# Column halves for the full-width products of layer-1 cross-attention, one more addition on GpSimd ahead of its sums, and four column groups for the layer-3 keys

## The chip, the cores and the metric

The kernel runs on one core of a Trainium2 chip. The metric is the time of one execution on the device, in microseconds (us), from the first to the last instruction and what lies around them; lower is better. The core has five engines with queues of their own: TensorE (PE in the profile; its weight loads are listed apart as PEld), VectorE (DVE), ScalarE (ACT), GpSimd (POOL) and SyncE (SP, which issues transfers).

## The reference, cut to what matters

The reference is a Perceiver-like stack of four layers, each with a cross-attention to a long context, a self-attention and a feed-forward part, on x of 2 x 256 x 256 and a context of 2 x 4096 x 256. The change touches two of its twelve parts, the cross-attentions of layers 1 and 3:

```python
def _L1_xattn_ref(input_query, input_key, input_value, Wq, bq, Wk, bk, Wv, bv, Wo, bo):
    q = jnp.einsum('bsd,hdk->bhsk', input_query, Wq) + bq[None, :, None, :]   # 16 heads of 64
    k = jnp.einsum('bsd,hdk->bhsk', input_key, Wk) + bk[None, :, None, :]
    v = jnp.einsum('bsd,hdv->bhsv', input_value, Wv) + bv[None, :, None, :]
    score = jax.nn.softmax(jnp.einsum('bhqk,bhsk->bhqs', q, k), axis=-1)
    z = jnp.einsum('bhqs,bhsv->bhqv', score, v)
    z = jnp.transpose(z, (0, 2, 1, 3)).reshape(z.shape[0], z.shape[2], -1)
    return z @ Wo + bo

x = x + _L1_xattn_ref(_layernorm(x), ctx, ctx, ...)      # ctx: 2 x 4096 x 256
x = x + _L3_xattn_ref(_layernorm(x), ctx, ctx, w_q, w_kv, w_concat)   # 16 query heads of 16, one key/value head
```

All of it is float32.

## The kernel before, in words

The kernel works through the parts one after the other. In **layer-1 cross-attention** (`l1_xattn`) the work is cut into 16 units u: two batches times eight pairs of heads. A pair of heads fills the 128 partitions (64 for each head). The 4096 context rows of a unit are cut into eight chunks of 512, so one loop runs over g = 8u + chunk, from -1 to 139, of which 0 to 127 are chunks. The code holds TensorE, VectorE, ScalarE and GpSimd to the order in which it is written (`in_order`), so one turn of the loop is a fixed sequence on each engine. It is a software pipeline: scores run for chunk g, their softmax weights for chunk g - 9, the product of weights and values for chunk g - 10.

One turn on TensorE, with the lines of the profile:

- `weigh` (L1098): weights times values, eight products of 256 columns. The two heads go to the two column halves of the array: each product has 128 rows and 64 columns (128\*64 in the profile), and its result goes to 64 of the 128 partitions of the bank `acc`.
- in the turn after a unit's last chunk (g % 8 == 1), the sums: a matrix of ones times `total`, in which GpSimd has collected the weights (L1086, L1088). `total` has two parts j for each head, so each head takes two products (4 in all). They go through the helper `mm` (L358).
- in other turns `out` (g % 8 == 2) or `query` (g % 8 == 5), also through L358.
- `keys` (L358, `ps_tr<-ctxT,w_l1x_wk`): two products over the full array of 128 rows and 128 columns, each of 512 columns.
- at a unit's boundary (g % 8 == 0) `turned` (L1119), four transposes that turn the maxima of the scores.
- `values` (L358, `ps_tr<-w_l1x_wv,ctxT`): eight full-array products of 128 columns.
- at a unit's boundary `repeat` (L1130), four transposes that spread the negated maxima. It needs `maxima` (L1125, VectorE), which needs `turned`.
- `scores` (L1051): eight products of 256 columns on 64 rows and 128 columns; the two heads go to the two row halves.

A float32 product stands in the trace as two MATMUL records and two LDWEIGHTS records; a transpose as one of each. "Moving" below is the operand that streams, "stationary" the one that is loaded into the array; the profile names the moving one first.

Beside it ScalarE copies scores out (L1058) and takes the exponential (L1075); VectorE takes the running maximum (L1061), adds the negated maximum (L1072) and copies values out (L335); GpSimd adds the weights into `total` (L1086). The last unit (u = 15) shares its additions between GpSimd and VectorE, with a second tile, `rest`. After the last chunk (g from 128) only `weigh` and `values` alternate until the weights of the last unit are used up.

In **layer-3 cross-attention** (`l3_xattn`) `key` (through L358) makes 512 columns of keys with two full-array products. It is one of a list of steps, `made`, that are put one by one between the scores of the first pass (L2172, on 32 rows and 128 columns; VectorE takes their maxima, L2176), two steps of scores to one of `made`, in a loop of 18 turns. All 16 `key` steps run before or in that loop. `value` beside it already runs in four column groups of 32 (L2134). In the main part that follows, weights (L2200) and their products with values (L2216) alternate with more of L2172.

Of the kernel before, what the change touches and what calls it, by code (L numbers as in the profile page):

```python
# [22 lines left out]
P = 128  # L23
B = 2
L = 256
# [4 lines left out]
KC = D // P  # L30
# [238 lines left out]
class Perceiver:  # L269
# [85 lines left out]
    def mm(self, out, pairs):  # L355

        for i, (lhsT, rhs) in enumerate(pairs):
            self.nc.tensor.matmul(out, lhsT, rhs, start=i == 0, stop=i == len(pairs) - 1)  # L358
# [614 lines left out]
    def l1_xattn(self, x, cpool):  # L973
# [9 lines left out]
        nc = self.nc  # L983
        with ExitStack() as s:
# [3 lines left out]
            xnT = self.to_T(self.layernorm(x))  # L988
            wq, wk, wv, wo = (self.weight(f"l1x_w{n}") for n in "qkvo")
# [6 lines left out]
            n = 8 * B  # L996
            G = 8 * n
            halves = [slice(0, 64), slice(64, 128)]
            order = [(hh, i) for i in range(2) for hh in range(2)]
            ctx, q, kT, v, score = {}, {}, {}, {}, {}  # L1000
            most, low, spread, total, av, sums, rec, z = {}, {}, {}, {}, {}, {}, {}, {}
# [7 lines left out]
            def for_values(g):  # L1009

                return ("k", g + 8) if g + 8 < G and (g + 8) // 64 == g // 64 else ("v", g)

            def query(u):
                ps = self.bank([P, L])
                self.mm(ps, [(wq[:, k, ts(u % 8, P)], xnT[:, k, ts(u // 8, L)]) for k in range(KC)])
                q[u] = p2.tile([P, L], F32, name="qT", tag="qT")
                return lambda: nc.vector.tensor_scalar_add(q[u], ps, self.col("l1x_bq", u % 8))

            def keys(g):
                pr = g // 8 % 8  # L1020
                ps = self.bank([P, 512], "tr")
                self.mm(ps, [(wk[:, k, ts(pr, P)], ctx["k", g][:, k, :]) for k in range(KC)])
                kT[g] = p2.tile([P, 512], F32, name="kT", tag="kT")
                nc.scalar.activation(kT[g], ps, AF.Identity, bias=self.col("l1x_bk", pr))

            def values(g):
                pr = g // 8 % 8
                ps = self.bank([P, 4, P], "tr")
                for i in range(4):
                    self.mm(  # L1030
                        ps[:, i, :],
                        [(ctx[for_values(g)][:, k, ts(i, P)], wv[:, k, ts(pr, P)]) for k in range(KC)],
                    )
                v[g] = p2.tile([P, 4, P], F32, name="v", tag="v", bufs=3)
                self.copy(g < G - 8, v[g], ps)
# [29 lines left out]
            def less(g, which):  # L1065

                u = g // 8
                if (g % 8, which[0]) == (0, order[0]):
                    total[u] = p2.tile([P, 2, 2, L], F32, name="total", tag="total")
                for hh, i in which:  # L1070
                    t = score[g][hh, i]
                    nc.vector.tensor_tensor(  # L1072
                        t, t, spread[u][:, hh, :].unsqueeze(1).to_broadcast([P, 2, L]), ALU.add
                    )
                    nc.scalar.activation(t, t, AF.Exp)  # L1075
                    tot = total[u][:, hh]
                    if u == n - 1 and hh == 1:

                        dst = tot if i == 0 else rest
                        src = (t,) if g % 8 == 0 else (dst, t)  # L1080
                        if i == 0:
                            (nc.gpsimd.tensor_add if g % 8 else nc.gpsimd.tensor_copy)(dst, *src)
                        else:
                            late.append(partial(nc.vector.tensor_add if g % 8 else nc.vector.tensor_copy, dst, *src))
                    elif g % 8 > 0:
                        nc.gpsimd.tensor_add(tot, tot, t)  # L1086
                    elif i == 1:
                        nc.gpsimd.tensor_add(tot, score[g][hh, 0], t)  # L1088

            def weigh(g):  # L1090
                u = g // 8
                if g % 8 == 0:
                    av[u] = self.acc([P, L])
                vs, got = v.pop(g), score.pop(g)
                for i in range(2):
                    for j in range(2):
                        for hh, part in enumerate(halves):
                            nc.tensor.matmul(  # L1098
                                av[u][part], vs[:, 2 * i + j, part], got[hh, i][:, j, :],
                                start=g % 8 == 0 and i + j == 0, stop=g % 8 == 7 and i + j == 2,  # L1100
                            )
                if g % 8 == 7:

                    sums[u] = self.bank([P, L])
                    for hh, part in enumerate(halves):
                        terms = [total[u][:, hh, j, :] for j in range(2)]
                        if u == n - 1 and hh == 1:
                            terms += [rest[:, j, :] for j in range(2)]
                        self.mm(sums[u][part], [(self.ones[:, 0:64], x) for x in terms])
# [6 lines left out]
            def turned(u):  # L1116
                ps = self.bank([P, 4, P])
                for i in range(4):
                    nc.tensor.transpose(ps[:, i, :], low[u][:, i // 2, ts(i % 2, P)], self.ident)  # L1119
                low[u] = ps  # L1120

            def maxima(u):
# [18 lines left out]
            def out(u):  # L1141
                ps = self.bank([P, 2, D])
                for qt in range(2):
                    self.mm(ps[:, qt, :], [(z[u][:, ts(qt, P)], wo[:, u % 8, :])])
                two = y[:, ts(u // 8, 2), :]
                return lambda: nc.vector.tensor_add(two, ps, two)

# [9 lines left out]
            with self.in_order(e.PE, e.DVE, e.Activation, e.Pool):  # L1157
                for g in range(-1, G + 12):
# [7 lines left out]
                    u = g // 8 - 1 if g % 8 == 0 and 0 < g <= G else None  # L1166
# [6 lines left out]
                    if g % 8 == 2 and made(g - 11):  # L1173
                        evacs.append(out((g - 11) // 8))
# [7 lines left out]
                    if made(g + 1):  # L1182
                        keys(g + 1)
# [8 lines left out]
                    if made(g - 9) and g <= G:  # L1192
                        values(g - 9)
                    if made(g - 8) and g >= G:
                        values(g - 8)
# [899 lines left out]
    def l3_xattn(self, x, cpool):  # L2095
# [9 lines left out]
        nc = self.nc  # L2105
        with ExitStack() as s:
# [3 lines left out]
            wk, wv, wq = self.weight("l3x_wk"), self.weight("l3x_wv"), self.weight("l3x_wq")  # L2110
# [3 lines left out]
            def keys(b):  # L2114

                cT = self.ctx_chunks(cpool, b, bufs=4)
                kT = kp.tile([P, NK], F32, name="kT", tag="kT")
                v = kp.tile([P, 2, 4, 4, 32], F32, name="v", tag="v")
                kv[b] = kT, v.rearrange("p u g i d -> p (u g i) d")
                vTs = {}  # L2120

                def key(j):
                    ps = self.bank([P, 512], "tr")
                    self.mm(ps, [(wk[:, k, :], cT[j // 2][:, k, ts(j % 2, 512)]) for k in range(KC)])
                    nc.scalar.activation(kT[:, ts(j, 512)], ps, AF.Identity, bias=self.col("lead"))

                def value(u):


                    ps = self.bank([P, 512], "tr")  # L2130
                    for k in range(KC):
                        for g in range(4):
                            j = 4 * u + g
                            nc.tensor.matmul(  # L2134
                                ps[ts(g, 32)], wv[:, k, :], cT[j // 2][:, k, ts(j % 2, 512)],
                                start=k == 0, stop=k == KC - 1,
                            )
                    vTs[u] = pool.tile([P, 512], F32, name="vT", tag="vT")
                    nc.scalar.activation(vTs[u], ps, AF.Identity, bias=self.col("behind"))

                def turned(u):
                    ps = self.bank([P, 4, P], "tr")
                    for i in range(4):
                        nc.tensor.transpose(ps[:, i, :], vTs[u][:, ts(i, P)], self.ident)
                    nc.scalar.copy(
                        v[:, u].rearrange("p g i d -> p i g d"), ps.rearrange("p i (g d) -> p i g d", d=32)
                    )

                return [partial(key, j) for j in range(8)] + [partial(f, u) for u in range(2) for f in (value, turned)]

            made = keys(0)
            xnT = self.to_T(self.layernorm(x))
            (qT,) = self.proj_heads(pool, "qT", wq, xnT)
            z = pool.tile([P, NT, D], F32, name="z")
# [435 lines left out]
```

## Time and profile before

| what | us |
|---|---|
| three runs | 2615.05, 2627.32, 2627.75 |
| their median | 2627.32 |
| profiled execution: its own time | 2616.86 |
| profiled execution: span from first to last instruction | 2615.1 |
| TensorE busy in the span | 2480.0 (95%) |
| VectorE, ScalarE, GpSimd busy | 1713.5, 1343.4, 919.3 |
| layer-1 cross-attention, roughly 290 to 1300 us of the span, TensorE busy in 366 to 940 us | 573.25 of 574.00 |
| layer-3 cross-attention, first pass (1925 to 1995 us), TensorE busy | 68.01 of 70.00 |

The span and the execution's own time differ by 1.8 us. The three runs lie 12.7 us apart, and the profiled execution lies beside the fastest of them. In a timeline, instructions of one line that follow each other are merged into one row: its first figure is the start of the first, its second the time from there to the end of the last, and xN is the number of records. The ends of matmuls are modelled and reach into the next row, so the time that a block takes is read from the start of one row to the start of the next.

### The profile page before, as it was taken

The page shows a single profiled execution, that of the slowest core. Times are in us where ns is not written, and L with a number is a line of the kernel's source. Part 1 is how long each engine was busy: PE and PEld are TensorE (multiplying, and loading weights), DVE is VectorE, ACT ScalarE, POOL GpSimd, SP SyncE. Part 2 cuts the span into 40 slices and gives each one's busy share as a digit, 9 for nine tenths or more (in the row PEclk, how much of TensorE's full clock was granted, in tenths as well). Part 3 has the DMA queues.
Part 4 walks back from the last instruction along what each step waited for, and adds up shares of the span by engine and source line. Part 5 has one row for each costly group of instructions (what it writes and reads, how often), then busy time and mean ns, then how long its engine had stood idle before and what let it go on. Part 6 is the DMA issues. An engine that isn't in the chain of part 4 may idle for free.

```text
span 2615.1 us, 45590 instructions
## 1 busy us (share of the span) xinstructions
PE 2480.0 (95%) x17701; PEld 1659.1 (63%) x17701; DVE 1713.5 (66%) x3184; ACT 1343.4 (51%) x2540; POOL 919.3 (35%) x864
## 2 busy tenths in 40 slices
PE   8987999999999999999799998899989999999889
PEld 6854566666666666666533565556935666664678
DVE  5566577777777777777769755544267888854642
ACT  3323666666666666666466421432215777784512
POOL 0520255555555555556639413001101222210010
PEclk9988999999999999999899998789999999999889
DMA  6210322222232222222210100005730000003656
GB/s 256 89 57 30 118 65 65 67 72 65 65 113 82 70 69 65 65 67 81 80 65 1 65 20 22 4 25 214 266 147 18 2 2 2 2 2 123 218 213 223
DMA packets 77255, 214.24 MB, mean 82 GB/s; under 512 B 6408, under 2 KB 21456, under 8 KB 66544
## 3 DMA queue, kind: packets, MB, share of 16 engines
q1 hardware_dynamic: 72128, 202.69, 23.4%
q0 software_dynamic: 1888, 5.90, 0.7%
q8 instruction: 139, 2.28, 0.4%
q10 hardware_dynamic: 3024, 2.75, 0.3%
q14 instruction: 76, 0.62, 0.1%
HBM read 190.48 MB, written 20.84 MB: 81 GB/s over the span
## 4 chain that ended last, share of the span: by engine, by line
PE 39%; DVE 6%; issue 2%; ACT 2%; POOL 2%; DMA 0%; another core or an unknown queue 0%; DVEq 0%; ACTq 0%; POOLq 0%; SPq 0%
PE ps_mm L358 10%; PE ps_mm L2172 5%; PE ps_tr L2216 5%; PE ps_tr L2200 4%; PE ps_tr L358 3%; PE acc L358 3%; PE ps_mm L785 2%; DVE state L1357 1%; POOL spread L1345 1%; PE ps_tr L2335 1%; PE acc L826 1%; PE ps_tr L801 1%; PE ps_tr L2378 1%; PE ps_mm L2360 1%; PE acc L1583 1%
## 5 line engine op out<-in xcount | busy, mean ns | idle before, releaser
L1086 POOL TENSOR_TENSOR total<-total,S 128x512 f32<-128x512 f32 x434 | 540.8, 1278 | 299.6 <-ACT S L1075 299.2
L1075 ACT ACTIVATE S<-S 128x512 f32<-128x512 f32 x512 | 302.3, 625 | 209.0 <-DVE S L1072 208.8
L2176 DVE TENSOR_REDUCE mx<-ps_mm 128x1 f32<-128x512 f32 x512 | 317.9, 684 | 73.0 <-PE ps_tr L2200 54.2
L1061 DVE TENSOR_TENSOR most<-ps_mm,most 128x512 f32<-128x512 f32 x448 | 278.3, 684 | 119.2 <-ACT S L1058 119.2
L1058 ACT COPY S<-ps_mm 128x512 f32<-128x512 f32 x512 | 262.8, 600 | 115.3 <-PE ps_mm L1051 114.5
L1072 DVE TENSOR_TENSOR S<-S,ps_dec 128x512 f32<-128x512 f32 x512 | 317.6, 680 | 1.3 <-PE ps_dec L1130 1.3
L2204 ACT ACTIVATE PT<-ps_tr 128x512 f32<-128x512 f32 x476 | 246.7, 603 | 74.6 <-PE ps_tr L2200 71.8
L358 PEld LDWEIGHTS ps_tr<-w_l1x_wv,ctxT 128*128 128x128 f32 x2048 | 246.9, 192 | 52.5 <-issue 52.2
L1051 PE MATMUL ps_mm<-qT,kT 64*128 64x256 f32 x2048 | 255.7, 389 | 0.0
L1098 PE MATMUL acc<-S,v 128*64 128x256 f32 x2048 | 250.1, 385 | 0.5 <-DVE rec L1136 0.4
L358 PE MATMUL ps_tr<-ctxT,w_l1x_wk 128*128 128x512 f32 x512 | 250.6, 612 | 0.0
L2172 PE MATMUL ps_mm<-kT,qT 32*128 32x512 f32 x1024 | 250.1, 618 | 0.2 <-DVE mx L2176 0.2
L358 PE MATMUL ps_tr<-w_l1x_wv,ctxT 128*128 128x128 f32 x2048 | 249.9, 275 | 0.0
L2200 PE MATMUL ps_tr<-qm,kT 32*128 32x256 f32 x1904 | 238.3, 388 | 0.0
L1051 PEld LDWEIGHTS ps_mm<-qT,kT 64*128 64x128 f32 x2048 | 187.3, 186 | 38.3 <-DVE most L1061 3.8
L1098 PEld LDWEIGHTS acc<-S,v 128*64 128x64 f32 x2048 | 136.1, 136 | 97.3 <-ACT S L1058 38.8
L2200 PEld LDWEIGHTS ps_tr<-qm,kT 32*128 32x128 f32 x1904 | 171.0, 184 | 15.6 <-issue 6.2
L2225 POOL TENSOR_TENSOR sums<-sums,part 128x256 f32<-128x256 f32 x102 | 73.7, 722 | 257.1 <-ACT part L2224 257.1
L358 PEld LDWEIGHTS ps_tr<-ctxT,w_l1x_wk 128*128 128x128 f32 x512 | 89.2, 189 | 100.6 <-issue 99.1
L335 DVE COPY v<-ps_tr 128x512 f32<-128x512 f32 x120 | 82.9, 690 | 89.0 <-PE ps_tr L358 88.9
L2216 PE MATMUL ps_tr<-PT,v 128*32 128x256 f32 x2048 | 139.6, 385 | 0.3 <-ACT PT L2204 0.3
L2172 PEld LDWEIGHTS ps_mm<-kT,qT 32*128 32x128 f32 x1024 | 86.3, 185 | 61.3 <-issue 49.9
(542 smaller groups left out, 3808.8 us busy)
## 6 DMA issues: line engine op xcount, KB each, us to landing
ctxT<-in_ctxT SPq DMA_DIRECT2D x144, 512.0 KB, 3.6
ctxT<-in_ctxT SPq DMA_DIRECT2D x16, 1024.0 KB, 5.7
w_l2f_gu<-in_l2f_gu SPq DMA_DIRECT2D x16, 1024.0 KB, 7.1
bd_dram<-bd SPq DMA_DIRECT2D x8, 1536.0 KB, 5.5
w_l3f_w<-in_l3f_w SPq DMA_DIRECT2D x11, 1028.0 KB, 9.8
w_l3f_w<-in_l3f_w SPq DMA_DIRECT2D x11, 1024.0 KB, 5.1
ctx<-in_ctx SPq DMA_DIRECT2D x8, 1024.0 KB, 4.9
w_l2f_down<-in_l2f_down SPq DMA_DIRECT2D x16, 512.0 KB, 5.3
```

Source lines behind the costliest of these rows:

```text
L358: self.nc.tensor.matmul(out, lhsT, rhs, start=i == 0, stop=i == len(pairs) - 1)
L1051: nc.tensor.matmul(banks[hh, i][:, j, :], k[part, ts(2 * i + j, P)], q[u][part, :], start=True, stop=True)
L1058: nc.scalar.copy(t, ps)
L1061: nc.vector.tensor_tensor(m, ps, m, ALU.max)
L1072: nc.vector.tensor_tensor(t, t, spread[u][:, hh, :].unsqueeze(1).to_broadcast([P, 2, L]), ALU.add)
L1075: nc.scalar.activation(t, t, AF.Exp)
L1086: nc.gpsimd.tensor_add(tot, tot, t)
L1098: nc.tensor.matmul(av[u][part], vs[:, 2 * i + j, part], got[hh, i][:, j, :], start=g % 8 == 0 and i + j == 0, stop=g % 8 == 7 and i + j == 2,)
L2172: nc.tensor.matmul(ps, qT[rows, 2 * half + c, ts(t, P)], kT[rows, ts(j, 512)], start=True, stop=True,)
L2176: nc.vector.tensor_reduce(mx[:, c, r, j : j + 1], ps, AX.X, ALU.max)
L2200: nc.tensor.matmul(ps[:, i, :], kT[rows, ts(2 * u + i, P)], q[rows], start=True, stop=True)
L2216: nc.tensor.matmul(ps[ts(r, 32), :], v[:, 2 * u + i, :], pt[:, i, :], start=i == 0, stop=i == 1)
```

## The change

Four edits; the order in which steps follow each other on each engine stays as it was.

- A new helper `mm` inside `l1_xattn` makes each product in two column halves of 64, one after the other, with the same moving operand. `query`, `keys`, `values` and `out` use it. The sums, `weigh`, `scores` and `repeat` stay as they were.
- `turned` no longer uses the transposing instruction: it makes an ordinary float32 product with the identity, in column halves.
- After the last addition of a unit's weights, for all units but the last, GpSimd adds the two parts of `total` together (128 partitions x 512 elements), and the sums of ones take one product for each head instead of two.
- In layer 3, `key` makes its keys in four column groups of 32, with the same moving operand.

```diff
+            def mm(ps, pairs):
+                for k, (a, b) in enumerate(pairs):
+                    for part in halves:
+                        nc.tensor.matmul(ps[part], a[:, part], b, start=k == 0, stop=k == len(pairs) - 1)
...
-                self.mm(ps, [(wk[:, k, ts(pr, P)], ctx["k", g][:, k, :]) for k in range(KC)])
+                mm(ps, [(wk[:, k, ts(pr, P)], ctx["k", g][:, k, :]) for k in range(KC)])
...
-                    self.mm(
+                    mm(
                         ps[:, i, :],
                         [(ctx[for_values(g)][:, k, ts(i, P)], wv[:, k, ts(pr, P)]) for k in range(KC)],
                     )
...
+                if g % 8 == 7 and which[-1] == order[-1] and u < n - 1:
+                    tot = total[u]
+                    nc.gpsimd.tensor_add(tot[:, :, 0, :], tot[:, :, 0, :], tot[:, :, 1, :])
...
-                        terms = [total[u][:, hh, j, :] for j in range(2)]
+                        terms = [total[u][:, hh, j, :] for j in range(1 if u < n - 1 else 2)]
...
-                    nc.tensor.transpose(ps[:, i, :], low[u][:, i // 2, ts(i % 2, P)], self.ident)
+                    mm(ps[:, i, :], [(low[u][:, i // 2, ts(i % 2, P)], self.ident)])
...
-                    self.mm(ps, [(wk[:, k, :], cT[j // 2][:, k, ts(j % 2, 512)]) for k in range(KC)])
+                    for k in range(KC):
+                        for r in range(4):
+                            nc.tensor.matmul(
+                                ps[ts(r, 32)], wk[:, k, ts(r, 32)], cT[j // 2][:, k, ts(j % 2, 512)],
+                                start=k == 0, stop=k == KC - 1,
+                            )
```

The lines for `query` and `out` change from `self.mm` to `mm` in the same way as those for `keys`.

More of the change, by code (lines that the diff above doesn't have):

```diff
@@ L1011, in for_values @@
                 return ("k", g + 8) if g + 8 < G and (g + 8) // 64 == g // 64 else ("v", g)
+            def mm(ps, pairs):
+                for k, (a, b) in enumerate(pairs):
+                    for part in halves:
+                        nc.tensor.matmul(ps[part], a[:, part], b, start=k == 0, stop=k == len(pairs) - 1)
             def query(u):
                 ps = self.bank([P, L])
-                self.mm(ps, [(wq[:, k, ts(u % 8, P)], xnT[:, k, ts(u // 8, L)]) for k in range(KC)])
+                mm(ps, [(wq[:, k, ts(u % 8, P)], xnT[:, k, ts(u // 8, L)]) for k in range(KC)])
                 q[u] = p2.tile([P, L], F32, name="qT", tag="qT")
@@ L1143, in out @@
                 for qt in range(2):
-                    self.mm(ps[:, qt, :], [(z[u][:, ts(qt, P)], wo[:, u % 8, :])])
+                    mm(ps[:, qt, :], [(z[u][:, ts(qt, P)], wo[:, u % 8, :])])
                 two = y[:, ts(u // 8, 2), :]
```

## The prediction

> **What bounds the kernel now.** I read the page first (busy shares, slices, granted clock), then the busy times by stretch, then TensorE's timeline through two turns of the layer-1 loop, then GpSimd's.
>
> ```profile
> PE   8987999999999999999799998899989999999889
> PEclk9988999999999999999899998789999999999889
> ```
>
> ```profile
> core 0: us, PE busy (x) PEld busy (x) DVE busy (x) ACT busy (x) POOL busy (x), PEclk, DMA share, GB/s
> 366.00:940.00 574.00, 573.25 (x3958) 397.11 (x3956) 428.90 (x689) 359.03 (x657) 335.58 (x270) 1.00 0.25 74
> ```
>
> Slices 6 to 19 are layer-1 cross-attention. TensorE never rests there (573.25 of 574.00 us), at full clock; the next engine, VectorE, is at 75%. What TensorE saves in a turn the loop saves, until another engine's chain is late. Busy does not mean useful, though, so I looked at the blocks:
>
> ```profile
> 999.78 0.65 PE L1130 MATMUL ps_dec<-ident,nm 128*128 128x128 f32 x4
> 1000.36 2.00 PE L1051 MATMUL ps_mm<-qT,kT 64*128 64x256 f32 x16
> 1002.29 1.95 PE L1098 MATMUL acc<-S,v 128*64 128x256 f32 x16
> 1004.07 1.08 PE L358 MATMUL ps_mm<-total,ones 128*64 128x256 f32 x8
> 1005.08 1.98 PE L358 MATMUL ps_tr<-ctxT,w_l1x_wk 128*128 128x512 f32 x4
> 1006.90 1.95 PE L358 MATMUL ps_tr<-w_l1x_wv,ctxT 128*128 128x128 f32 x16
> 1008.78 2.00 PE L1051 MATMUL ps_mm<-qT,kT 64*128 64x256 f32 x16
> 1010.71 1.95 PE L1098 MATMUL acc<-S,v 128*64 128x256 f32 x16
> 1012.58 1.13 PE L358 MATMUL ps_mm<-w_l1x_wo,zT 128*128 128x256 f32 x4
> 1013.55 1.88 PE L358 MATMUL ps_tr<-ctxT,w_l1x_wk 128*128 128x512 f32 x4
> 1015.27 1.95 PE L358 MATMUL ps_tr<-w_l1x_wv,ctxT 128*128 128x128 f32 x16
> ```
>
> Take start-to-start times. `weigh` before the sums, which have the same 128\*64 shape: 1004.07 - 1002.29 = 1.78. `weigh` before `out`, 128\*128: 1012.58 - 1010.71 = 1.87. Leaving a shape costs 0.09. `keys` after the sums (new shape): 1006.90 - 1005.08 = 1.82; after `out` (same shape): 1015.27 - 1013.55 = 1.72. Entering 128\*128 costs 0.10. So a change of array shape costs about 0.19 to 0.20 us, and each regular turn has three: `values` to `scores`, `scores` to `weigh`, `weigh` to the rest.
>
> **What the Trainium skill says.** "TensorEngine Tiling (Array Packing)", Key Properties: changing the tiling mode, not just the tile, drains the TensorE. The trace agrees: 0.09 on leaving, nothing where the shape stays. "TensorE: Matmul & The Clock Gate", section LDWEIGHTS: a load takes columns / 1.2 ns, so 107 ns for 128, 53 for 64, 27 for 32. After a drain the first load cannot hide, which is the 0.10 on entry. The same page, Part 3: products in different column groups run together. `weigh` agrees: 16 records of 256 columns in 1.78 us is 0.22 for a pair; four full-array records (`out`) take 0.97 us, 0.24 each. Of halves with a common moving operand neither page nor trace has an instance: in `weigh`, the sums and L2216 every group has its own. "TensorEngine Tiling (Array Packing)", Restrictions, has column tiling exclude the float32 transpose mode; no run here shows it, and it fits that `turned` becomes a plain product.
>
> **The change part by part**, layer 1 first.
>
> *Switch out of `weigh`.* With column halves, all between `weigh` and `scores` has its shape. It goes in the turns g = 10 to 127, 118 of them. In 14 (g = 16, 24, ... 120) nothing is won, see below. 104 x 0.197 (0.09 + 0.10, matmul by matmul 0.093 + 0.104) = **-20.5**. The other two switches stay. In the ten turns before g = 10, `keys` follows `scores`: the switch stays, only its first load is shorter, 10 x 0.05 = **-0.5**.
>
> *Rate inside the blocks.* Same columns streamed, in pairs: `keys` stays at four times 0.43. `values` becomes 32 records, two in the time of one, 16 x 0.11. Can TensorE issue that fast, with a load each? Layer 3 has the instance, in the chain:
>
> ```profile
> 2489.09 1.88 PE acc L2390 x64
> ```
>
> 64 records of 128 columns in four groups: 29 ns each, where the halves of `values` need 55. Within that block a set of four takes 109 ns, a record of `values` now 112. I take 0.03 for each of the 104 turns, **-3** (bounds 0 and -4).
>
> *The unit's boundary* (g % 8 == 0). `repeat` waits for `maxima`: from the last `values` record to `repeat` there are 0.25 us beyond the record's own time, in every unit. It is VectorE's queue that is late (the additions L1072 stand ahead of the reduction), counted from the scores of the turn before. Hence: `weigh` to `keys` -0.20, `values` -0.03, but `turned` becomes 16 half records, eight pairs of 0.11, where four took 0.44: +0.44. Net +0.21 into a gap of 0.25: hidden. `values` to `repeat` is now a switch: its drain of 0.09 overruns the rest by 0.05. 14 x 0.05 = **+0.7** (bounds 0 and +2 with a full exposed load).
>
> *The sums.* 2 x 2 products less their half: eight records become four. Two pairs fewer at 0.216 = -0.43 for a unit. The price is on GpSimd:
>
> ```profile
> 998.14 4.96 POOL L1086 TENSOR_TENSOR total<-total,S 128x512 f32<-128x512 f32 x4 [3.27 <-ACT S L1075]
> ```
>
> The last addition ends at 1003.10, the sums start at 1004.07: 0.97 to spare, the same within 0.01 in all 14 units before the last two. The new addition has the size of an L1086 (512 elements in each partition; 1278 ns on the page) and follows at once: end 1004.37. From GpSimd's end to a waiting sum the trace has 0.05 (the last unit). So the sums start at 1004.43, 0.36 late, and their first load, now unhidden, adds 0.05. Both ends are counted from VectorE's chain (`repeat` and the exponentials), so the quicker TensorE changes nothing in it. Queued behind the sum on TensorE are the turn's `keys`, `values` and `scores`, so 0.41 is lost in full: 14 x (0.41 - 0.43) = **-0.3**. Halving the sums thus gives nothing. VectorE's reciprocal, which waits for the sums, comes no later; the next unit's GpSimd work starts 6.40 after the old end (L1088's wait), room enough for 1.27.
>
> *The tail* (g from 128). TensorE saves some 2.4 there (six switches into `values` at 0.2, seven out of it at 0.15), but it isn't what ends last:
>
> ```profile
> 1292.39 1.09 PE L358 MATMUL ps_mm<-total,ones 128*64 128x256 f32 x8 [3.62 <-POOL total L1086]
> ```
>
> GpSimd's queue is nearly unbroken from 1262.8 to 1292.3. The sums of unit 14 (1256.41) have only 0.1 to spare, so the new addition pushes them by 1.27 - 0.43 = 0.84, with VectorE's reciprocal and the additions behind it; GpSimd has gaps of 0.39 and 0.38 to win back a part. **+0.5** (bounds -2.4 and +1.3).
>
> *Layer 3.* `key` lies between scores of shape 32\*128, so both switches stay; its first load falls from 128 columns to 32. `key` 1927.18 - 1925.27 = 1.91 against `value`, already in four groups, 1.85:
>
> ```profile
> 1925.27 1.98 PE L358 MATMUL ps_tr<-ctxT,w_l3x_wk 128*128 128x512 f32 x4
> 1927.18 1.83 PE L2172 MATMUL ps_mm<-kT,qT 32*128 32x512 f32 x8
> 1945.26 1.92 PE L2134 MATMUL ps_tr<-ctxT,w_l3x_wv 128*32 128x512 f32 x16
> 1947.11 1.89 PE L2172 MATMUL ps_mm<-kT,qT 32*128 32x512 f32 x8
> ```
>
> 14 keys in the loop x 0.06 = **-0.8**; the two ahead of it gain a switch to and from 128\*128, under VectorE's layer norm (bounds 0 and -1.5).
>
> Sum: -20.5 - 0.5 - 3 + 0.7 - 0.3 + 0.5 - 0.8 = **-23.9**. The profiled execution took 2616.86 (span 2615.1 plus 1.8): 2616.9 - 23.9 = 2593.0. The runs before lie in two places, one at 2615 and two at 2627; the profile belongs to the low one, the median to the high. I expect a median in the high place again: 2627.3 - 23.9 = **2603**. That is 0.9%; about 0.5% (13 us) is what a measurement of this kernel can tell from no change.
>
> **Rivals.**
>
> *A. The common moving operand* (slower). Halves of `keys` and `values` read the same addresses in the same instant. If the second half has to wait for the first, the pair takes the time of two. For it: no instance in the trace. Against it: pairs and fours with operands of their own run at full rate. Break-even: 23.9 / 118 turns = 0.20 of the 3.5 us that `keys` and `values` take, 6% lost overlap. With no overlap 118 x 3.5 = +413: 2603 + 413 = 3016. Chance 0.12.
>
> *B. GpSimd's wait* is dearer: beside VectorE its additions took up to 1.73 in the tail (1278 on the mean). 0.46 more for each of 14 units, +6.4, and +1 in the tail: 2611. Chance 0.08.
>
> *C. The switch is not one.* If the 0.20 belongs to the change of operation and not of shape, it stays: only -3 and small terms, 2623. Against it: `weigh` to sums and `out` to `keys` change operation at no cost. Chance 0.06.
>
> **How the numbers follow.** Forecast 0.74. Low end: the low place with the favourable bounds (-31): 2584; high: the high place with about -14, which takes in B: 2614. A and C, 0.18, are left out. Faster by over 0.5%: forecast and most of B, 0.80. Within 0.5%: C and the rest of B, 0.08. Slower: A, 0.12.
>
> **What would show it.** In the changed profile `keys` should start 1.78 after `weigh`, not 1.87, and last 1.72 in every turn; a turn without `query`, `out` or sums should last 0.23 less; `repeat` should still start on VectorE's word; the sums should show a wait for GpSimd of about 0.4 in each unit. If `keys` or `values` last longer than now, A is at work. I'd be wrong too if VectorE or ScalarE ended last in the shorter turn.

## The result, and the profile after

| | before | after |
|---|---|---|
| runs (us) | 2615.05, 2617.16, 2617.87, 2621.22, 2627.32, 2627.75 | 2597.83, 2598.88, 2599.37, 2600.52, 2601.84, 2603.53 |
| median | 2619.55 | 2599.94 |
| profiled execution: span | 2615.1 | 2598.4 |

The ratio is 0.992 with a 95% interval of 0.9901 to 0.9938: 16 to 26 us faster. The forecast was 2603 in a range of 2584 to 2614. Three of the runs before are new; they lowered its median by 8 us.

The page of the changed kernel first (the rows of busy shares and of the granted clock): nothing else than TensorE has become the bound. From 366 to 920 us, within layer-1 cross-attention, it is busy for 552.14 of 554.00 us at a granted clock of 1.00.

```profile
PE   8987999999999999999799998899989999999889
PEclk9988999999999999999899998889999999998889
```

A regular turn on TensorE before (one without `query`, `out`, sums or boundary; start, length, engine, line, result and operands, shape, records):

```profile
1017.14 2.00 PE L1051 MATMUL ps_mm<-qT,kT 64*128 64x256 f32 x16
1019.07 1.95 PE L1098 MATMUL acc<-S,v 128*64 128x256 f32 x16
1020.95 1.98 PE L358 MATMUL ps_tr<-ctxT,w_l1x_wk 128*128 128x512 f32 x4
1022.77 1.95 PE L358 MATMUL ps_tr<-w_l1x_wv,ctxT 128*128 128x128 f32 x16
1024.65 2.00 PE L1051 MATMUL ps_mm<-qT,kT 64*128 64x256 f32 x16
```

And the changed kernel, from a unit's boundary over two turns, then (behind the dots) a regular one:

```profile
980.47 1.04 PE L1017 MATMUL ps_mm<-ident,low 128*64 128x128 f32 x16
981.34 1.92 PE L1017 MATMUL ps_tr<-w_l1x_wv,ctxT 128*64 128x128 f32 x32
983.18 0.65 PE L1139 MATMUL ps_dec<-ident,nm 128*128 128x128 f32 x4
983.77 2.00 PE L1057 MATMUL ps_mm<-qT,kT 64*128 64x256 f32 x16
985.69 1.95 PE L1107 MATMUL acc<-S,v 128*64 128x256 f32 x16
987.87 0.65 PE L358 MATMUL ps_mm<-total,ones 128*64 128x256 f32 x4 [0.23 <-POOL total L1097]
988.35 1.89 PE L1017 MATMUL ps_tr<-ctxT,w_l1x_wk 128*64 128x512 f32 x8
990.07 1.92 PE L1017 MATMUL ps_tr<-w_l1x_wv,ctxT 128*64 128x128 f32 x32
991.91 2.00 PE L1057 MATMUL ps_mm<-qT,kT 64*128 64x256 f32 x16
...
1000.05 2.00 PE L1057 MATMUL ps_mm<-qT,kT 64*128 64x256 f32 x16
1001.97 1.95 PE L1107 MATMUL acc<-S,v 128*64 128x256 f32 x16
1003.75 1.89 PE L1017 MATMUL ps_tr<-ctxT,w_l1x_wk 128*64 128x512 f32 x8
1005.47 1.92 PE L1017 MATMUL ps_tr<-w_l1x_wv,ctxT 128*64 128x128 f32 x32
1007.32 2.00 PE L1057 MATMUL ps_mm<-qT,kT 64*128 64x256 f32 x16
```

Read it from start to start again. In the regular turn `weigh` to `keys` is 1003.75 - 1001.97 = 1.78 (1.88 before), `keys` lasts 1.72 (1.82), `values` to `scores` 1007.32 - 1005.47 = 1.85 (1.88), the whole turn 1007.32 - 1000.05 = 7.27 (7.51 in the rows above, 7.50 in the median over the units). In the turn of the sums these start 987.87 - 985.69 = 2.18 after `weigh` instead of 1.78: they are 0.40 late. They take 988.35 - 987.87 = 0.48. With the halves alone and whole sums (`halves_only` below) they take 0.86, and the `values` behind them 0.05 longer: what is won is 0.43, hardly more than the 0.40 that is lost. The row of the sums writes only 0.23 of the delay down as a wait, as the modelled ends of `weigh` reach into it; starts are the safer reading. GpSimd's timeline has the cause:

```profile
981.50 4.97 POOL L1092 TENSOR_TENSOR total<-total,S 128x512 f32<-128x512 f32 x4 [3.02 <-ACT S L1081]
986.54 1.27 POOL L1097 TENSOR_TENSOR total<-total 128x512 f32<-128x512 f32 x1
```

The new addition ends at 987.81 and the sums start at 987.87; in each of the 15 units with the new addition they start 0.05 to 0.06 after its end.

Where the time went, by part of the program (from the first TensorE record of each part to that of the next, in the profiled executions):

| part | before | after | difference |
|---|---|---|---|
| ahead of layer-1 cross-attention | 260.8 | 261.3 | +0.6 |
| layer-1 cross-attention, to the last scores | 985.3 | 961.6 | -23.7 |
| its tail | 61.1 | 62.5 | +1.4 |
| layer-1 state-space part (not touched) | 200.2 | 203.1 | +2.9 |
| from there to layer 3 (not touched) | 405.6 | 405.6 | 0 |
| layer-3 cross-attention | 451.5 | 450.6 | -0.9 |
| layer-3 self-attention (not touched) | 159.9 | 163.0 | +3.2 |
| the rest | 90.7 | 90.6 | 0 |

The touched parts give -23.2; between 6 and 7 us come back where no instruction was changed. The busy times of an untouched stretch point to the clock: layer-3 self-attention, before and after (stretch, its length, busy time of each engine, granted clock, share and rate of transfers):

```profile
2364.50:2524.40 159.90, 136.91 (x846) 92.06 (x847) 87.56 (x306) 62.71 (x136) 10.04 (x18) 0.83 0.46 160
```

```profile
2344.70:2507.80 163.10, 139.90 (x847) 94.63 (x848) 87.57 (x306) 62.74 (x136) 10.03 (x18) 0.81 0.46 160
```

VectorE, ScalarE and GpSimd have the same busy time to 0.03 us; TensorE needs 3 more at a granted clock of 0.81 instead of 0.83. Over all ten profiles of this study the untouched parts differ by as much: the layer-1 state-space part takes 199.9 to 200.3 in four of them and 202.3 to 203.1 in six, layer-3 self-attention 159.9 in the one of before and 162.2 to 164.6 in the other nine. The profile of before had drawn short ones.

### The profile page after: what moved, and what is told of

It reads as the page before. It is cut to its first block, busy times and chain, and to the rows that moved or that the text cites. A ratio compares the mean times of both kernels' runs of the same rounds, so it can differ in the third digit from the quotient of the medians.

```text
span 2598.4 us, 51704 instructions
## 1 busy us (share of the span) xinstructions
PE 2456.6 (95%) x20711; PEld 1625.2 (63%) x20713; DVE 1711.5 (66%) x3184; ACT 1342.4 (52%) x2540; POOL 940.5 (36%) x879
## 4 chain that ended last, share of the span: by engine, by line
PE 40%; DVE 6%; ACT 2%; issue 2%; POOL 2%; DMA 0%; DVEq 0%; ACTq 0%; POOLq 0%; SPq 0%
PE ps_mm L358 10%; PE ps_mm L2187 5%; PE ps_tr L2231 5%; PE ps_tr L2215 4%; PE acc L358 3%; PE ps_tr L358 2%; PE ps_mm L785 2%; DVE state L1366 1%; PE ps_tr L2136 1%; POOL spread L1354 1%; PE ps_tr L2350 1%; PE acc L826 1%; PE ps_tr L2393 1%; PE ps_tr L801 1%; PE acc L1592 1%
## 5 line engine op out<-in xcount | busy, mean ns | idle before, releaser
L1017 PEld LDWEIGHTS ps_tr<-w_l1x_wv,ctxT 128*64 128x64 f32 x4096 | 233.9, 137 | 59.9 <-issue 59.1
L1017 PE MATMUL ps_tr<-w_l1x_wv,ctxT 128*64 128x128 f32 x4096 | 247.5, 273 | 0.0
L1017 PE MATMUL ps_tr<-ctxT,w_l1x_wk 128*64 128x512 f32 x1024 | 242.1, 594 | 0.0
L1017 PEld LDWEIGHTS ps_tr<-ctxT,w_l1x_wk 128*64 128x64 f32 x1024 | 73.0, 137 | 94.3 <-issue 77.3
```

The source lines that it names most:

```text
L1017: nc.tensor.matmul(ps[part], a[:, part], b, start=k == 0, stop=k == len(pairs) - 1)
```

## The experiments

Eight kernels. Those with medians ran beside the kernel before on the same chip; the others have one time and a profile. Turns of the loop, from the start of one `scores` to the next (medians over the units, to 0.01 us):

| kernel | time | regular turn | boundary turn | sums turn | last scores to last sums |
|---|---|---|---|---|---|
| before | 2619.55 | 7.50 | 8.68 | 8.42 | 46.3 |
| after | 2599.94 | 7.27 | 8.72 | 8.15 | 47.5 |
| halves_only | 2599.65 | 7.27 | 8.72 | 8.18 | 47.2 |
| sums_only | 2624.16, once | 7.50 | 8.68 | 8.43 | 47.2 |
| values_only | 2635.39 | 7.62 | 8.68 | 8.53 | 48.5 |
| keys_only | 2623.36, once | 7.50 | 8.68 | 8.42 | 46.3 |
| sums_later | 2591.24 | 7.27 | 8.72 | 7.70 | 46.3 |
| turned_whole | 2595.40, once | 7.27 | 8.68 | 8.20 | 47.5 |
| l3_keys_only | 2625.38, once | 7.50 | 8.68 | 8.42 | 46.3 |
| later_and_whole | 2591.83 | 7.27 | 8.68 | 7.70 | 45.6 |

Single times are no better than the spread of the runs, some 12 us; the turns, which repeat to 0.01 or 0.02, carry those verdicts. The kernel before took 2619.71 beside `halves_only`, `values_only` and `sums_later` and 2623.77 beside `later_and_whole`, so medians are compared by their ratio to it. The last column ends at the first record of the last unit's sums. Of its figures 48.5 is no effect of the edit alone: in the profile of `values_only` the granted clock was 0.50 for 3.4 us early in that stretch, while in the other nine it stayed at 1.00 until TensorE had only those sums left to wait for.

**Is it the halves or the sums?** First the halves alone. The edit against the changed kernel:

```diff
-                if g % 8 == 7 and which[-1] == order[-1] and u < n - 1:
-                    tot = total[u]
-                    nc.gpsimd.tensor_add(tot[:, :, 0, :], tot[:, :, 0, :], tot[:, :, 1, :])
-                        terms = [total[u][:, hh, j, :] for j in range(1 if u < n - 1 else 2)]
+                        terms = [total[u][:, hh, j, :] for j in range(2)]
```

and `key` of layer 3 as before.

> Only the column halves of layer 1; the sums take two products for each head again, with no further addition on GpSimd, and the layer-3 keys are whole. If the gain is the shape switch out of weigh, and halving the sums gives back on GpSimd what it saves, the regular turn lasts 7.27 us as in the changed kernel, the turn with the sums 8.13, with no wait for GpSimd, and the time is the changed kernel's within 2 us (2600). If the shorter sums do bring their 0.43 us in each of 14 units, it is 6 us slower than the changed kernel (2606).

It took 2599.65, ratio to before 0.9918 (0.9895 to 0.9941), the changed kernel's 2599.94. (The expectations write 8.13 and 8.37 for the turn of the sums; these are the turns with `out` and `query`. The turn of the sums has 8.15 and 8.42.) The sums start 1.78 after `weigh`, without a wait, and take 0.86:

```profile
984.80 1.95 PE L1104 MATMUL acc<-S,v 128*64 128x256 f32 x16
986.58 1.08 PE L358 MATMUL ps_mm<-total,ones 128*64 128x256 f32 x8
987.44 1.94 PE L1017 MATMUL ps_tr<-ctxT,w_l1x_wk 128*64 128x512 f32 x8
```

The column halves of layer 1 are the whole gain. The sums alone, on the kernel before (the same three added lines and `range`, no halves):

> The kernel before with only GpSimd's further addition and the halved sums. If the addition makes the sums wait as long as they get shorter, the turn with the sums stays at 8.37 us, of which about 0.4 is a wait for GpSimd, and the time is the one before within 1.5 us. If the halved products count, that turn falls to 7.94 and the layer-1 part loses 6 us.

The turn of the sums is 8.43 against 8.42. They start 1003.73 - 1001.51 = 2.22 after `weigh`, 0.44 later than before, for 0.43 saved. In the tail they come 0.9 later than before (47.2 against 46.3). The whole layer-1 part has 1047.8 against 1046.4, but it has 1047.7 in `l3_keys_only` too, which leaves it alone.

**Shape or operation?** Half of the change, on the kernel before: `mm` in `values` alone.

```diff
-                    self.mm(
+                    mm(
                         ps[:, i, :],
                         [(ctx[for_values(g)][:, k, ts(i, P)], wv[:, k, ts(pr, P)]) for k in range(KC)],
                     )
```

> The kernel before with column halves in values alone. If the cost belongs to changes of shape, a turn gains a switch (keys to values, 0.09 + 0.05) and keeps the three it had: 7.50 becomes 7.62 us, 104 turns give +12 us, 2632 against 2620. If it belongs to changes of operation, or if halves are quicker in themselves, the turn is at or below 7.50 and the time the one before or less.

2635.39, ratio 1.0055 (1.0032 to 1.0078): slower, at 7.62 us a turn. Up to the last scores the layer-1 part takes 997.3 instead of 985.3, the 12 us that were expected; 2.8 more lie in its tail, where the clock was low. Its timeline:

```profile
1022.88 1.88 PE L358 MATMUL ps_tr<-ctxT,w_l1x_wk 128*128 128x512 f32 x4
1024.69 1.97 PE L1017 MATMUL ps_tr<-w_l1x_wv,ctxT 128*64 128x128 f32 x32
1026.59 2.00 PE L1057 MATMUL ps_mm<-qT,kT 64*128 64x256 f32 x16
```

`keys`, here behind `out`, now last 1.81 to the next start instead of 1.72 (the drain), `values` 1.90 instead of 1.87 (0.05 for the first load, less the 0.03 of the quicker rate). The counterpart, `mm` in `query`, `keys` and `out` (the diff has the lines), `turned` and `values` whole:

> The kernel before with column halves in keys, query and out alone; turned and values stay whole. If the cost belongs to changes of shape, the switch of 0.20 us is not removed but moved from in front of keys to in front of values, and the turn stays at 7.50 us and the layer-1 part at 1046 within 2. If the halves of keys and query are quicker in themselves, or the switch belongs to the end of weigh, the turn falls to about 7.3.

The turn is 7.50 to the hundredth:

```profile
1020.52 2.00 PE L1057 MATMUL ps_mm<-qT,kT 64*128 64x256 f32 x16
1022.45 1.95 PE L1104 MATMUL acc<-S,v 128*64 128x256 f32 x16
1024.23 1.89 PE L1017 MATMUL ps_tr<-ctxT,w_l1x_wk 128*64 128x512 f32 x8
1026.04 2.05 PE L358 MATMUL ps_tr<-w_l1x_wv,ctxT 128*128 128x128 f32 x16
1028.03 2.00 PE L1057 MATMUL ps_mm<-qT,kT 64*128 64x256 f32 x16
```

`weigh` to `keys` falls from 1.88 to 1.78. `keys` to `values` stays at 1.81 to 1.82: the first load of `keys` costs nothing now, but the shape is left behind it. `values` rises from 1.88 to 1.99. The switch has moved by one block. One half of the edit loses 0.12 a turn, the other gives nothing, both together give 0.23. That is what a cost of changes of shape makes of them, and nothing else that was proposed does; rival C falls.

**Can the sums be made to pay?** On the changed kernel, the sums moved:

```diff
                     if made(g + 1):
                         keys(g + 1)
+                    if made(g - 10) and g % 8 == 1:
+                        add_up((g - 10) // 8)
...
                         less(g - 9, order[2:])
+                    if made(g - 10) and g % 8 == 1:
+                        end((g - 10) // 8)
```

`add_up` is the block of the sums from `weigh`; the two lines with `end` stand behind the second `less` and no longer ahead of `keys`.

> The changed kernel with the sums moved behind the keys of the same turn, and the reciprocal behind VectorE's second pair of additions, so that GpSimd's further addition is done when the sums come up. If the wait of 0.4 us for GpSimd in each unit is all that the halved sums lack, the turn with the sums falls from 8.13 to 7.70 and the time by 6 us to 2594. If another wait takes its place (the last bank of the scores must then wait for the later reciprocal), the turn stays at 8.1 or gets longer.

2591.24, ratio to before 0.9899 (0.9871 to 0.9927). The turn of the sums is 7.70:

```profile
980.57 1.95 PE L1107 MATMUL acc<-S,v 128*64 128x256 f32 x16
982.35 1.89 PE L1017 MATMUL ps_tr<-ctxT,w_l1x_wk 128*64 128x512 f32 x8
984.07 0.60 PE L358 MATMUL ps_mm<-total,ones 128*64 128x256 f32 x4
984.50 1.92 PE L1017 MATMUL ps_tr<-w_l1x_wv,ctxT 128*64 128x128 f32 x32
```

No wait; the sums take 0.43. GpSimd's addition has ended 1.36 before. The 0.45 of each unit (6.3 for 14) were lost to this wait and to the first load that it left unhidden (0.05).

**The boundary.** `turned` by whole transposes again in the changed kernel:

```diff
-                    mm(ps[:, i, :], [(low[u][:, i // 2, ts(i % 2, P)], self.ident)])
+                    nc.tensor.transpose(ps[:, i, :], low[u][:, i // 2, ts(i % 2, P)], self.ident)
```

> The changed kernel with turned made by whole transposes again: two switches more on TensorE at a unit's boundary (0.29 us with their loads) for 0.44 us of products less. If the boundary turn is set by VectorE's maxima, the turn falls only by what overran, from 8.72 to 8.68 us. If TensorE sets it, it falls by 0.15 to 8.57.

The boundary turn fell to 8.68 as expected, so VectorE's maxima do set it. But nothing was won: the turn of the sums behind it rose from 8.15 to 8.20.

```profile
983.85 1.95 PE L1107 MATMUL acc<-S,v 128*64 128x256 f32 x16
986.07 0.65 PE L358 MATMUL ps_mm<-total,ones 128*64 128x256 f32 x4 [0.28 <-POOL total L1097]
```

2.22 from `weigh` to the sums, where the changed kernel has 2.18. GpSimd's end is counted from VectorE's chain and stays where it is, so what TensorE gains ahead of the sums it waits longer. Its one time of 2595.40 is within the spread.

**Layer 3.** The four column groups of `key`, alone, on the kernel before (the last hunk of the diff):

> The kernel before with the four column groups of the layer-3 keys alone. If only the load behind the switch gets shorter, a key takes 1.85 us instead of 1.91 and the first pass of layer 3 loses about 1 us; all else stays. If four streams of one moving operand disturb each other, a key takes longer than 1.91.

```profile
1936.50 1.92 PE L2127 MATMUL ps_tr<-ctxT,w_l3x_wk 128*32 128x512 f32 x16
1938.35 1.14 PE L2178 MATMUL ps_mm<-kT,qT 32*128 32x512 f32 x8
1939.42 1.92 PE L2127 MATMUL ps_tr<-ctxT,w_l3x_wk 128*32 128x512 f32 x16
1941.28 1.89 PE L2178 MATMUL ps_mm<-kT,qT 32*128 32x512 f32 x8
1943.10 1.92 PE L2127 MATMUL ps_tr<-ctxT,w_l3x_wk 128*32 128x512 f32 x16
```

A key takes 1.85 as expected, but the gain halves: every second block of scores grew from 1.76 to 1.82, as it waits for VectorE to free a bank (in the one that starts at 1941.28, the last quarter of the scores starts at 1942.05, and the maxima of the block before last until 1941.99). Two keys with their scores take 1943.10 - 1936.50 = 6.60 where before they took 1931.93 - 1925.27 = 6.66. That is about 0.4 for the 14 keys of the loop. In the whole part it can't be told from the differences between executions: 450.5 here, 451.5 before, 450.9 to 451.3 in four more kernels that left layer 3 alone, and 450.6 to 452.5 in the four others with the groups.

**All three costs mended**: the sums moved, the further addition for units up to 13 only, `turned` whole.

```diff
-                if g % 8 == 7 and which[-1] == order[-1] and u < n - 1:
+                if g % 8 == 7 and which[-1] == order[-1] and u < n - 2:
-                        terms = [total[u][:, hh, j, :] for j in range(1 if u < n - 1 else 2)]
+                    terms = [total[u][:, hh, j, :] for j in range(1 if u < n - 2 else 2)]
```

> The changed kernel with the sums behind the keys, GpSimd's further addition left out for unit 14 too (its two products stay), and turned by whole transposes. If the three costs that the changed kernel kept are the wait of the sums, the push on GpSimd's last stretch and the overrun at the boundary, this gives 6 + 1 + 0.7 us against the changed kernel: about 2592, and a boundary turn of 8.68 us with a sums turn of 7.70. If the tail is set by TensorE or VectorE instead, its stretch from the last scores to the end of the part stays as it is with the sums moved alone.

2591.83, ratio to before 0.9882 (0.9864 to 0.99): with `sums_later` the best of the study, about 8 us below the changed kernel, and not to be told apart from `sums_later` by time. In the trace all three show: boundary turn 8.68, sums turn 7.70, last scores to last sums 45.6 instead of 47.5 (46.3 with the sums moved alone). The layer-1 part takes 1015.2 us, against 1016.3 with the sums moved alone, 1024.1 in the changed kernel and 1046.4 before.

## Why the prediction was right, step by step

**The base.** I took the higher of two places, 2627. With more runs there are not two places but a row of steps, and the median before is 2619.55; 2619.55 - 23.9 = 2595.7 would have been the forecast, and 2599.94 was measured. So that 2603 lies within 4 us of the result is partly luck: the base was 7.8 too high, and the gain in the medians is 19.6 (16 to 26) and not 23.9, and the two errors work against each other. The profile of before, on which the sum was built, has short draws of the untouched parts; three kernels whose loop runs at or near the old speed (`sums_only`, `keys_only`, `l3_keys_only`) have spans of 2621.6 to 2623.6 for its 2615.1. The low end of the range was reckoned with -31; the favourable bounds given for the single terms add up to -29.2, which makes it 2586.

**The switch out of `weigh`, the early turns and the rate**: forecast -0.23 for a regular turn, measured 7.50 to 7.27. Up to the last scores I had -20.5 - 0.5 - 3 + 0.7 - 0.3 = -23.6; the part measures -23.7. Right, and `values_only` with `keys_only` show it for the reason given. The agreement to 0.1 is luck, though: the 118 turns from g = 10 on gave 24.2 where 23.1 had been reckoned. The ten early turns gave nothing instead of 0.5: 0.05 each was won in most of them, but at the first boundary (g = 8), where no `values` stand between `turned` and `repeat`, the longer `turned` cost 0.46. The way to the first scores took 0.4 more in this execution (-0.1 and +0.2 in two other kernels with the halves).

**The boundary**: +0.05 forecast, 8.68 to 8.72 measured, hidden by VectorE as stated. What I missed: the overrun costs nothing while the sums behind it wait for GpSimd (`turned_whole`). Two waits that hang on the same chain must not be added.

**The sums**: forecast 0.41 lost for 0.43 won; measured 0.40 for 0.43 in the changed kernel (8.18 without it, 8.15 with it), 0.44 for 0.43 on its own.

**The tail**: forecast +0.5, bounds to +1.3; from the last scores to the last sums it measured +1.2, to the next part +1.4. This is the term that was mis-sized. The step that failed is that only unit 14's addition was counted, with a part of it won back in GpSimd's gaps. The rows before, then after: `turned`, `repeat` and unit 14's sums on TensorE, and GpSimd's first addition for the last unit after these sums.

```profile
1250.06 0.63 PE L1119 MATMUL ps_mm<-ident,low 128*128 128x128 f32 x4 [1.73 <-DVE low L1114]
1254.10 0.60 PE L1130 MATMUL ps_dec<-ident,nm 128*128 128x128 f32 x4
1256.41 1.08 PE L358 MATMUL ps_mm<-total,ones 128*64 128x256 f32 x8
1261.08 1.28 POOL L1088 TENSOR_TENSOR total<-S 128x512 f32<-128x512 f32 x1 [3.65 <-ACT S L1075]
```

```profile
1227.16 1.09 PE L1017 MATMUL ps_mm<-ident,low 128*64 128x128 f32 x16 [1.97 <-DVE low L1123]
1231.68 0.65 PE L1139 MATMUL ps_dec<-ident,nm 128*128 128x128 f32 x4
1234.79 0.65 PE L358 MATMUL ps_mm<-total,ones 128*64 128x256 f32 x4 [0.59 <-POOL total L1097]
1239.04 1.28 POOL L1094 TENSOR_TENSOR total<-S 128x512 f32<-128x512 f32 x1 [3.75 <-ACT S L1081]
```

The last record of scores stands at 1246.09 and at 1222.94. Counted from there, GpSimd's addition starts at 15.0 before and 16.1 after, and its last sums are late by about as much (46.3 and 47.5). It waits for ScalarE's exponentials; these stand in ScalarE's queue behind `zT`, which needs VectorE's reciprocal, which needs the sums.

The runs separate the two causes. The addition alone (`sums_only`) makes this start 15.9 and the last sums 0.9 later: the push of 0.84 was right, but nothing of it was won back. The halves alone (`halves_only`) make it 15.8 and the last sums 0.85 later: at this boundary TensorE waits for VectorE's `low`, then has `turned` and two blocks of `values` on the path. `turned` starts 0.2 later after the last scores, and from `turned` to `repeat` it takes 4.5 us instead of 4.0. Both delays go through the same sums, so they do not add. `turned_whole` agrees: 4.2 from `turned` to `repeat`, but the sums still wait for the addition, and the last sums stay at 47.5. With the sums and the reciprocal moved (`sums_later`) the exponentials no longer stand behind `zT`, and the stretch is back at 46.3 with both causes still in.

**Layer 3**: forecast -0.8, about -0.4 in the loop. The load got shorter as stated, but I counted all of it on the path, where VectorE takes back half of it.

**Rivals.** A, the common moving operand, falls: `keys` last 1.72 with two streams of one operand, the layer-3 keys 1.85 with four, where `value` with four operands has the same 1.85. B: the addition took 1.27 to 1.28 in all 15 units, not 1.73. C fell above.

## What to carry to other kernels

On a busy engine look for the price of transitions: compare one block's start-to-start time by what follows and what precedes it. Count changes of array shape in a turn of the loop and take them away for the whole run between two that must stay; half of such an edit can cost more than none. A cheaper product gains nothing if its input is made later: before adding work ahead of a consumer, read how much slack the producer has, and move the consumer if there is none.

## What the runs showed of the hardware

- Two or four column groups that stream the same addresses at once run at the full rate (`keys` 1.72 us for eight half records of 512 columns, as for four whole ones; a layer-3 key 1.85 in four groups, as `value` with four operands). The Trainium skill ("TensorE: Matmul & The Clock Gate", Part 3) says that tiles run concurrently and doesn't speak of a common operand; here it does no harm.
- Leaving a shape costs 0.093 to 0.100 us, read from start to start, matmul by matmul, in layer-1 cross-attention. The first product after entering one takes 0.101 to 0.104 longer where the load has 128 columns, 0.051 for 64 and 0.023 to 0.026 for 32. So it is in all ten profiles; where the next block has the same shape neither is there (0.00).
- Parts that no edit touched differ by about 3 us between executions (199.9 to 203.1, 159.9 to 164.6); in the two executions compared above the other engines' busy time was unchanged and the granted TensorE clock 0.81 instead of 0.83. That is half of what `sums_later` won in its turns (6.3), so changes of this size are read from the turns.
